# Latent cross-attention on Trainium2: maxima carried into the next pass, and weights prepared through GpSimd's queue

## The chip, the cores and the metric

The kernel runs on one core of one Trainium2 chip. The metric is the device time of one execution in microseconds (us), the median of several runs. The core's engines are TensorE (PE; PEld is its weight load), VectorE (DVE), ScalarE (ACT), GpSimd (POOL) and SyncE (SP), which here only issues DMAs. Each engine works through its own queue in order and waits on semaphores.

## The reference

One layer with 512 latent tokens of width 512 and a context of 8192 tokens: a layer norm and cross-attention with 16 heads of 64, then a state-space block with its gated MLP, then a mixture of 16 experts with two chosen per token and a shared expert. The change concerns the cross-attention and the weights that later parts need:

```python
q = (scale * (Q @ Wq + bq)).reshape(bs, q_len, NH, DM)
k = (K @ Wk + bk).reshape(bs, kv_len, NH, DM)
v = (V @ Wv + bv).reshape(bs, kv_len, NH, DM)
qk = jnp.einsum('nlhd,nshd->nhls', q, k)
a = jax.nn.softmax(qk, axis=-1)
o = jnp.einsum('nhls,nshd->nlhd', a, v).reshape(bs, q_len, NH * DM)
return o @ Wo + bo
```

All inputs are float32. The kernel keeps each factor as two float16 parts, high and low, and multiplies three of the four products.

## The kernel before

The heads are taken in eight pairs, two pairs to a pass, so four passes. A pass goes over the context in 16 chunks of 512 tokens. Per chunk it projects K for both pairs (kproj_units, tile psk, L250 to L252) and V (vproj_units, tile psv, L274 to L276), stores them to device memory (k_d, v_d), and one chunk later computes coarse scores (smax_units, tile psx, L297), which ACT brings to sf (L302) and DVE folds into a running maximum runm (L310). At the end of a pass maxrow_units reduces runm (L317, L318), transposes it on PE (tile ptm, L321), and writes its negative as an extra row of the query tile (mrow, L323, L325).

The attention itself runs in units: a pair of heads and half of the queries, 16 units of 32 steps. A step (scores, then av) takes 256 context tokens: eight matmuls for scores (L359, L360), exponentials on ACT (L367, L369, or in every second step a cast on DVE, L371), the low part by a subtraction on DVE (tile phl, L372, once per step), and the products with V (L389, L392) one or two steps later.

The first pass runs alone. The other three passes are a generator, filler(), whose pieces are woven between the steps of the units before. Every piece yields its nominal cost in ns, and advance() takes pieces until a target is reached: start + LEAD + (n + 0.5) * rate, and again with n + 1.0, where n is the step. So LEAD is how much of the next pass is done before the first step, and rate how much per step. PASSN is the nominal cost of one pass, 223640 ns. Inside filler(), side is a list of score generators, and pump() takes one piece from the first of them, after every second projection piece (every fourth in the first pass). At the end of a pass, before, the list is emptied at once:

```python
            while side:
                yield from pump()
            mr = [maxrow_units(p, runm[i]) for i, p in enumerate(pr)]
            for x in mr:
                yield next(x)
```

The rest of maxrow_units runs in the next pass's first chunk. The order of PE's instructions is the order in which the program writes them. For the other engines and the DMA queues a scheduler of the compiler decides the order, from its own estimate of when each instruction's inputs are ready.

weight_prep() runs beside all this. It first stores zeros to the expert buffers (23 stores to xd_d, L513, and five to y_d, L515), then prepares 52 blocks of weights for the later parts. A block is one load of 512 KB (tile mpf, two buffers, L522) and two halves. Each half is scaled to the high part (L535) and to the low part (L536) on DVE into the tile mph and stored (256 KB, L537). Every second step takes one piece of it. The mph tiles share four buffers (tag t2k) with zero and the projected queries. All these DMAs are issued by SP, whose queue also has the context loads (ctxc, L242), the K and V stores (k_d, L260; v_d, L283) and the loads of K and V for the steps (k, kb, v, L338 to L342).

Steps over NFILL use a second pair of PSUM buffers for scores. The last unit runs beside the beginning of the later parts (tail()).

Of the kernel before, what the change touches and what calls it, by code (L numbers as in the profile page):

```python
# [8 lines left out]
F16 = mybir.dt.float16  # L9
# [7 lines left out]
P = 128  # L17
# [4 lines left out]
CH = 512  # L22
# [7 lines left out]
NPASS = NPAIR // 2  # L30
NDC = NCH // 2
HQ = NQ // 2
NSTEP = 32
PASSN = 16 * (4 * 2592 + 8 * 406) + 2 * 2592 + 600


@with_exitstack
def perceiver_layer(ctx: ExitStack, tc: tile.TileContext, a: dict, out: bass.AP):
    nc = tc.nc
# [96 lines left out]
    sb2 = R(attn, "a2", 2)  # L136
# [146 lines left out]
        nc.sync.dma_start(v_d[g][c // 2][:, tt : tt + 2], vs)  # L283
        yield 648

    def smax_units(c, qh, kh, runm, wide):

        for q2 in range(2):
            sf = sb3.tile([P, 2, 2, CH], F16, name="sf", bufs=2)
            pss = []  # L290
            for qi in range(2):
                qt = 2 * q2 + qi
                for hh in range(2):
                    s = slice(hh * 64, hh * 64 + 64)
                    pool, tag = (ps_s, "pss") if wide and qi else (ps_x, "px")
                    ps = pool.tile([P, CH], F32, name="psx", tag=tag)
                    nc.tensor.matmul(ps, lhsT=qh[s, qt * P : (qt + 1) * P], rhs=kh[s, 0, :], start=True, stop=True)  # L297
                    pss.append((sf[:, qi, hh, :], ps))
                if wide and not qi:
                    continue  # L300
                for dst, ps in pss:
                    nc.scalar.activation(dst, ps, AF.Copy, scale=1.0 / (8.0 * WS))  # L302
                pss = []
                if not qi:
                    yield 406
            r = runm[:, 2 * q2 : 2 * q2 + 2]
            if c == 0:
                nc.vector.tensor_copy(r, sf)
            else:
                nc.vector.tensor_tensor(r, r, sf, ALU.max)  # L310
            yield 626 if wide else 406

    def maxrow_units(p, runm):
        qlm = state[p]["q"][1]
        m = sb2.tile([P, 2, 4], F32, name="mx")
        for w in (256, 128):
            nc.vector.tensor_tensor(runm[:, :, :, 0:w], runm[:, :, :, 0:w], runm[:, :, :, w : 2 * w], ALU.max)  # L317
        nc.vector.tensor_reduce(m.rearrange("p h q -> p q h"), runm[:, :, :, 0:128], axis=AX.X, op=ALU.max)  # L318
        yield 0
        pt = bank_j([P, P], F32, "ptm")  # L320
        nc.tensor.transpose(pt[0:8, :], m.rearrange("p h q -> p (h q)"), ident)  # L321
        r = sb2.tile([8, P], F16, name="mrow")
        nc.scalar.activation(r, pt[0:8, :], AF.Copy, bias=PSHIFT, scale=-1.0)  # L323
        for hh in range(2):
            nc.sync.dma_start(  # L325
                qlm[64:65, hh, :].rearrange("o (a b) -> o a b", b=P), r[hh * 4 : hh * 4 + 4, :]
            )
        state[p]["ready"] = True
        yield 300
# [91 lines left out]
    def filler():  # L421
        side = []

        def pump():
            while side:
                u = next(side[0], None)
                if u is not None:
                    yield u
                    break
                side.pop(0)  # L430

        def pass_weights(g):
            pr = (2 * g, 2 * g + 1)
            out = []
            for src, n, tag, bufs in (
                (a["Wk"][pr[0]], P, "k", 4), (a["Wk"][pr[1]], P, "k", 4), (a["Wv"][g], 256, "v", 2),
                (a["Wq"][pr[0]], P, "q", 2), (a["Wq"][pr[1]], P, "q", 2),
            ):
                w = stage_w(src, n, tag, bufs=bufs)
                yield None  # L440
                out.append(w())
            yield out[0:2], out[2], out[3:5]

        mr, nw = [], None
        for g in range(NPASS):
            pr = (2 * g, 2 * g + 1)
            if g == 0:
                wk0 = load_w(a["Wk"][0], P, "k", bufs=4)
                nct = ctx_first(0)
                wk = [wk0, load_w(a["Wk"][1], P, "k", ("p32", 3), bufs=4)]  # L450
                wv = load_w(a["Wv"][0], 256, "v", ("p32", 3))
                nc.sync.dma_start(x_sb, a["x"])
                wq = [load_w(a["Wq"][p], P, "q", ("t2k", 4)) for p in pr]
            else:
                wk, wv, wq = nw
                qh = [qproj(p, w) for p, w in zip(pr, wq)]
                yield 2 * 2592
            runm = [sb2.tile([P, 4, 2, CH], F16, name=f"runm{i}", tag=f"runm{i}", bufs=1) for i in range(2)] if g else None
            ks = [[None] * NCH for _ in pr]
            for c in range(NCH):  # L460
                if c == NCH - 7 and g < NPASS - 1:
                    nws = pass_weights(g + 1)
                if c >= NCH - 7 and g < NPASS - 1:
                    nw = next(nws, None) or nw
                ct = nct
                nxt = g * NCH + c + 1
                if nxt < NPASS * NCH:
                    nct = ctx_first(nxt) if nxt < NCH else ctx_load(nxt % NCH)
                gens = [kproj_units(p, c, ct, wk[i], ks[i]) for i, p in enumerate(pr)]
                gens += [vproj_units(g, c, ct, wv, j) for j in range(2)]  # L470
                k = 0
                for n, gen in enumerate(gens):
                    for u in gen:
                        yield u
                        k += 1
                        if k % (2 if g else 4) == 0:
                            yield from pump()
                    if mr and c == 0:
                        yield from mr.pop(0)
                if g == 0 and c == 0:  # L480
                    first_norm()
                    qh = [qproj(p, w) for p, w in zip(pr, wq)]
                    yield 2 * 2592
                    runm = [sb2.tile([P, 4, 2, CH], F16, name=f"runm{i}", tag=f"runm{i}", bufs=1) for i in range(2)]
                if c == 2:
                    for p, q in zip(pr, qh):
                        qplace(p, *q)
                side += [smax_units(c, qh[i][0], ks[i][c], runm[i], g == 0) for i in range(2)]
            while side:
                yield from pump()  # L490
            mr = [maxrow_units(p, runm[i]) for i, p in enumerate(pr)]
            for x in mr:
                yield next(x)
            if g == NPASS - 1:
                for x in mr:
                    yield from x
            passes[0] = g + 1

    fill = filler()
# [9 lines left out]
    def weight_prep():  # L509
        zero = sb2.tile([P, 2 * DM], F16, name="zero", tag="t2k", bufs=4)  # L510
        nc.gpsimd.memset(zero, 0.0)
        for k in range(16 + NOV):
            nc.sync.dma_start(xd_d[k * P : (k + 1) * P, :], zero)  # L513
            if k >= 16 + MOV:
                nc.sync.dma_start(y_d[k * P : (k + 1) * P, :], zero.bitcast(F32))  # L515
            if k % 4 == 3 or k == 15 + NOV:
                yield
        blocks = [(name, i, dst) for name in mlp_d for i, dst in enumerate(mlp_d[name])]

        def fetch(j):  # L520
            f = sb2.tile([P, 1024], F32, name="mpf", bufs=2)
            nc.sync.dma_start(f, a[blocks[j][0]][:, blocks[j][1]])  # L522
            return f

        nf = fetch(0)
        yield
        for j, (name, i, dst) in enumerate(blocks):
            f = nf
            if j + 1 < len(blocks):
                nf = fetch(j + 1)  # L530
            yield
            for h in range(2):
                sl = slice(h * 512, h * 512 + 512)
                hl = sb2.tile([P, 2, 512], F16, name="mph", tag="t2k", bufs=4)
                nc.vector.tensor_scalar(hl[:, 0], f[:, sl], WF, None, ALU.mult)  # L535
                nc.vector.scalar_tensor_tensor(hl[:, 1], f[:, sl], WF, hl[:, 0], ALU.mult, ALU.subtract)  # L536
                nc.sync.dma_start(dst[:, :, sl], hl)  # L537
                yield

    ms = ExitStack()  # L540
# [1 line left out]

    units = [(p, h) for p in range(NPAIR) for h in range(2)]
    NLAST = len(units) - 1
    LEAD = 11500
    loads = {}

    def load(j):
# [7 lines left out]
    load(0)  # L556
    advance(start + LEAD)
    load(1)
    pend, enders, early = [], [], weight_prep()
    NFILL = 12 * NSTEP - 4  # L560
    rate = (NPASS - 1) * PASSN / NFILL
    sp = (sb2, sb3, 3)
    po = []

# [10 lines left out]
    for n in range(NLAST * NSTEP):  # L575
# [10 lines left out]
        while len(pend) > (2 if m == 2 else 1):  # L586
            drain()
        advance(start + LEAD + (n + 1.0) * rate)
        pend.append((u, m, cur))
# [769 lines left out]
```

## Time and profile before

| | us |
|---|---|
| median of 3 runs | 2652.26 (2648.97 to 2652.97) |
| profiled execution | 2653.45 |
| its span, first to last instruction | 2651.7 |
| PE busy | 2410.6 (91%) |
| DVE busy | 2049.4 (77%) |
| ACT busy | 1955.5 (74%) |
| POOL busy | 44.2 (2%) |

The granted clock of TensorE has a mean of 0.959 over the span. In the execution that was profiled the first pass ends and the second begins at about 250 us, passes three and four begin near 695 and 1165, and the last projection matmul of pass four starts at 1605; steps run from 278 us. In tables by stretch a row gives a stretch of time, its length, then busy time and number of instructions of each engine, then the granted clock (1.00 is full), the mean busy share of the 16 DMA engines and the rate they moved in GB/s. An idle time in brackets is that of the engine just before the instruction, with what ended it.

### The profile page before, as it was taken

Reading aid. Unit: us, or ns where it says so; the run is one execution under the profiler, and the core shown is the slowest. Engines: PE = TensorE matmul, PEld = TensorE weight load, DVE = VectorE, ACT = ScalarE, POOL = GpSimd, SP = SyncE. Lnnn points to the kernel's source line nnn. Section 1 sums busy time; section 2 is a strip of 40 time slices with the busy share of each in tenths; the row PEclk is TensorE's granted clock in tenths of the full one; section 3 lists DMA queues with packets and bytes.
Section 4 is the critical chain, followed back from the end, with each engine's and each line's share of the span. In section 5 each row is a group of like instructions: output and inputs, shape, how many; then the busy total and the mean of one; then the engine's idle time right before and its main releaser. Section 6 shows DMA issues by size and latency. Waiting matters only on the chain. (4 is left out here: it accounts for less than half of the span.)

```text
span 2651.7 us, 54346 instructions
## 1 busy us (share of the span) xinstructions
PE 2410.6 (91%) x21806; PEld 1693.5 (64%) x21806; DVE 2049.4 (77%) x2403; ACT 1955.5 (74%) x3734; POOL 44.2 (2%) x58
## 2 busy tenths in 40 slices
PE   7999998999999899998999998998878688998895
PEld 4454676777666677766677766997656466665442
DVE  6876688877877877777877777997899999633785
ACT  5787787888787788867788887997868476432784
POOL 2000000000000000000000000000000000001001
PEclk9999999999899999989999998999989889999998
DMA  7973899866598866658966655887511322675896
GB/s 265 308 255 128 268 284 270 242 169 187 166 268 264 265 189 176 184 152 250 253 176 190 173 162 129 201 204 206 171 56 41 96 72 82 229 233 200 294 337 222
DMA packets 353686, 531.42 MB, mean 200 GB/s; under 512 B 25106, under 2 KB 218834, under 8 KB 353300
## 3 DMA queue, kind: packets, MB, share of 16 engines
q1 hardware_dynamic: 352148, 523.69, 65.6%
q0 software_dynamic: 1280, 4.20, 0.5%
q8 instruction: 173, 2.83, 0.5%
q14 instruction: 85, 0.70, 0.1%
HBM read 397.68 MB, written 126.94 MB: 198 GB/s over the span
## 5 line engine op out<-in xcount | busy, mean ns | idle before, releaser
L372 DVE TENSOR_TENSOR phl<-p,phl 128x1024 f16<-128x1024 f32 x512 | 625.9, 1224 | 175.0 <-ACT phl L369 158.9
L367 ACT ACTIVATE p<-pss 128x512 f32<-128x512 f32 x1024 | 596.8, 619 | 126.1 <-PE pss L360 50.7
L302 ACT ACTIVATE sf<-psx 128x512 f16<-128x512 f32 x1024 | 557.7, 622 | 79.1 <-PE psx L297 77.2
L359 PE MATMUL pss<-qhh,k 128*128 128x256 f16 x2048 | 486.2, 277 | 18.5 <-ACT phl L369 18.0
L360 PE MATMUL pss<-qlm,kb 128*128 128x256 f16 x2048 | 485.2, 276 | 0.6 <-DMA kb<-k_d 0.4
L389 PE MATMUL po<-v,phl 128*128 128x130 f16 x4096 | 327.2, 222 | 5.2 <-DVE oq L402 4.7
L310 DVE TENSOR_TENSOR runm<-runm,sf 128x2048 f16<-128x2048 f16 x240 | 292.4, 1218 | 45.7 <-ACT sf L302 45.2
L389 PEld LDWEIGHTS <-phl 128*128 128x128 f16 x4096 | 273.9, 99 | 69.4 <-issue 21.5
L369 ACT ACTIVATE phl<-pss 128x512 f16<-128x512 f32 x512 | 312.3, 610 | 0.0
L274 PE MATMUL psv<-wh_v,ctxc 128*128 128x256 f16 x1024 | 283.4, 277 | 7.7 <-DVE khl L258 3.4
L275 PE MATMUL psv<-wl_v,ctxc 128*128 128x256 f16 x1024 | 282.2, 276 | 1.2 <-DVE wl_v L176 1.2
L276 PE MATMUL psv<-wh_v,ctxc 128*128 128x256 f16 x1024 | 282.1, 276 | 0.0
L359 PEld LDWEIGHTS <-k 128*128 128x128 f16 x2048 | 202.2, 99 | 63.7 <-issue 18.0
L360 PEld LDWEIGHTS <-kb 128*128 128x128 f16 x2048 | 202.7, 99 | 61.0 <-issue 22.2
L297 PE MATMUL psx<-khl,qh 64*128 64x512 f16 x1024 | 212.5, 395 | 21.3 <-ACT sf L302 18.4
L371 DVE CAST phl<-p 128x1024 f16<-128x1024 f32 x256 | 176.1, 688 | 58.1 <-ACT p L367 57.7
L392 PE MATMUL po<-v,phl 128*128 128x65 f16 x4096 | 209.9, 194 | 9.3 <-DVE phl L372 9.3
L250 PE MATMUL psk<-ctxc,wh_k 128*128 128x512 f16 x512 | 198.6, 388 | 21.1 <-DVE vs L281 10.5
L919 PE MATMUL py<-hs,ident 128*128 128x256 f32 x512 | 148.1, 447 | 67.1 <-DVE hs L916 67.0
L251 PE MATMUL psk<-ctxc,wh_k 128*128 128x512 f16 x512 | 197.2, 385 | 0.7 <-DVE ctxc L234 0.7
L252 PE MATMUL psk<-ctxc,wl_k 128*128 128x512 f16 x512 | 196.8, 384 | 0.0
L392 PEld LDWEIGHTS <-phl 128*128 128x128 f16 x4096 | 172.8, 98 | 12.8 <-DVE phl L372 12.0
(304 smaller groups left out, 3711.9 us busy)
## 6 DMA issues: line engine op xcount, KB each, us to landing
v<-v_d SPq DMA_DIRECT2D x128, 520.0 KB, 4.4
k<-k_d SPq DMA_DIRECT2D x256, 256.0 KB, 5.8
ctxc<-ctx_d SPq DMA_DIRECT2D x96, 512.0 KB, 5.2
wef<-in_gu_dram SPq DMA_DIRECT2D x72, 512.0 KB, 5.9
v_d<-vs SPq DMA_DIRECT2D x128, 260.0 KB, 3.8
k_d<-khl SPq DMA_DIRECT2D x128, 256.0 KB, 4.2
kb<-k_d SPq DMA_DIRECT2D x128, 256.0 KB, 5.4
wpm<-w_d SPq DMA_DIRECT2D x48, 512.0 KB, 3.9
```

What stands on the lines that cost most here:

```text
L274: nc.tensor.matmul(ps[:, t, :], lhsT=ct[i // 2][:, 0, i % 2, sl], rhs=wh[:, i, :], start=i == 0, stop=False)
L275: nc.tensor.matmul(ps[:, t, :], lhsT=ct[i // 2][:, 0, i % 2, sl], rhs=wl[:, i, :], start=False, stop=False)
L276: nc.tensor.matmul(ps[:, t, :], lhsT=ct[i // 2][:, 1, i % 2, sl], rhs=wh[:, i, :], start=False, stop=i == NC4 - 1)
L302: nc.scalar.activation(dst, ps, AF.Copy, scale=1.0 / (8.0 * WS))
L310: nc.vector.tensor_tensor(r, r, sf, ALU.max)
L359: nc.tensor.matmul(ps[:, hh], lhsT=k[:, hh, sl], rhs=qhh[:, hh, qs], start=True, stop=False)
L360: nc.tensor.matmul(ps[:, hh], lhsT=b[:, hh, sl], rhs=qlm[:, hh, qs], start=False, stop=True)
L367: nc.scalar.activation(p32[:, i], pss[i], AF.Exp, scale=sc)
L369: nc.scalar.activation(ph[:, i], pss[i], AF.Exp, scale=sc)
L372: nc.vector.tensor_tensor(pl, p32, ph, ALU.subtract)
L389: nc.tensor.matmul(o, lhsT=ph[:, i, hh, qs], rhs=vv, start=first, stop=False, **kw)
L392: nc.tensor.matmul(o, lhsT=pl[:, i, hh, qs], rhs=vv_, start=False, stop=last, **kw)
```

## The change

The drain at the end of a pass is gone: what is left in side, and the two maxrow_units, are carried into the next pass, where one piece is pumped after every projection piece as long as more than two generators wait. runm is allocated by the first score piece of a pass that uses it, since the old maxima may still be in use when the new pass begins. maxrow_units gives three empty pieces between its reduction and its transpose. After the last pass the remaining pieces are spread by LAST / 10 ns each. LEAD rises from 11500 to 27500, NFILL falls by two, and rate follows from both: 1765.6 before, 1723.3 ns per step after. The loads and stores of the weight blocks are issued by GpSimd; the zeros stay with SP. No instruction of PE, DVE or ACT is added or removed.

```diff
+LAST = 8000
...
-    def smax_units(c, qh, kh, runm, wide):
-
+    def smax_units(c, i, qh, kh, runm, wide):
+
+        if c == 0:
+            runm[i] = sb2.tile([P, 4, 2, CH], F16, name=f"runm{i}", tag=f"runm{i}", bufs=1)
...
-            r = runm[:, 2 * q2 : 2 * q2 + 2]
+            r = runm[i][:, 2 * q2 : 2 * q2 + 2]
...
-    def maxrow_units(p, runm):
+    def maxrow_units(p, i, runm):
+        runm = runm[i]
...
-        yield 0
+        for _ in range(3):
+            yield 0
         pt = bank_j([P, P], F32, "ptm")
...
-        mr, nw = [], None
+        nw = None
...
-            runm = [sb2.tile([P, 4, 2, CH], F16, name=f"runm{i}", tag=f"runm{i}", bufs=1) for i in range(2)] if g else None
+            runm = [None, None]
...
                     for u in gen:
                         yield u
                         k += 1
-                        if k % (2 if g else 4) == 0:
+                        if k % (2 if g else 4) == 0 or len(side) > 2:
                             yield from pump()
-                    if mr and c == 0:
-                        yield from mr.pop(0)
...
-                side += [smax_units(c, qh[i][0], ks[i][c], runm[i], g == 0) for i in range(2)]
-            while side:
-                yield from pump()
-            mr = [maxrow_units(p, runm[i]) for i, p in enumerate(pr)]
-            for x in mr:
-                yield next(x)
+                side += [smax_units(c, i, qh[i][0], ks[i][c], runm, g == 0) for i in range(2)]
+            side += [maxrow_units(p, i, runm) for i, p in enumerate(pr)]
             if g == NPASS - 1:
-                for x in mr:
-                    yield from x
+                while side:
+                    yield from pump()
+                    yield LAST / 10
...
-            nc.sync.dma_start(f, a[blocks[j][0]][:, blocks[j][1]])
+            nc.gpsimd.dma_start(f, a[blocks[j][0]][:, blocks[j][1]])
...
-                nc.sync.dma_start(dst[:, :, sl], hl)
+                nc.gpsimd.dma_start(dst[:, :, sl], hl)
...
-    LEAD = 11500
+    LEAD = 27500
...
-    NFILL = 12 * NSTEP - 4
-    rate = (NPASS - 1) * PASSN / NFILL
+    NFILL = 12 * NSTEP - 6
+    rate = ((NPASS - 1) * PASSN + LAST - LEAD) / NFILL
```

More of the change, by code (lines that the diff above doesn't have):

```diff
@@ L483, in filler @@
                     yield 2 * 2592
-                    runm = [sb2.tile([P, 4, 2, CH], F16, name=f"runm{i}", tag=f"runm{i}", bufs=1) for i in range(2)]
                 if c == 2:
```

## The prediction

> **What bounds the kernel now.** I read the page first, then the busy time by stretch, then the same stretches for one line that runs once per step, then the waits of VectorE and the order of time around one of them. The page says that TensorE (PE) is the engine to watch:
>
> ```profile
> PE 2410.6 (91%) x21806; PEld 1693.5 (64%) x21806; DVE 2049.4 (77%) x2403; ACT 1955.5 (74%) x3734; POOL 44.2 (2%) x58
> ```
>
> The busy time by stretch shows where PE is not full. I cut at the places where the three fill passes begin and end (columns: PE, PEld, DVE, ACT, POOL busy, granted clock, DMA share, GB/s):
>
> ```profile
> 250.00:278.00 28.00, 25.84 (x115) 11.68 (x115) 20.02 (x26) 13.91 (x28) 0.00 (x0) 0.82 0.29 105
> 278.00:500.00 222.00, 213.78 (x2171) 153.20 (x2170) 180.58 (x228) 181.02 (x353) 0.00 (x0) 0.98 0.92 280
> 500.00:675.00 175.00, 174.72 (x1823) 126.87 (x1822) 131.68 (x147) 151.12 (x298) 0.00 (x0) 1.00 0.65 182
> 675.00:700.00 25.00, 20.57 (x145) 11.12 (x143) 19.66 (x19) 19.24 (x37) 0.00 (x0) 0.73 0.44 128
> 700.00:925.00 225.00, 206.72 (x2088) 148.36 (x2085) 181.17 (x250) 164.67 (x322) 0.00 (x0) 0.97 0.85 256
> ...
> 1150.00:1175.00 25.00, 22.88 (x162) 12.61 (x161) 19.52 (x24) 15.73 (x30) 0.00 (x0) 0.73 0.34 86
> 1175.00:1325.00 150.00, 136.35 (x1375) 98.82 (x1373) 114.91 (x156) 107.71 (x210) 0.00 (x0) 0.97 0.89 249
> 1325.00:1600.00 275.00, 274.06 (x2875) 200.34 (x2874) 204.46 (x227) 234.49 (x462) 0.10 (x1) 1.00 0.63 175
> 1600.00:1632.00 32.00, 24.11 (x196) 15.73 (x195) 23.94 (x24) 22.30 (x45) 2.19 (x5) 0.73 0.32 82
> ```
>
> The same stretches for L372 alone (one per step) give the pace:
>
> ```profile
> 278.00:500.00 222.00, 75.47 (x62) 0.98 0.92 280
> 500.00:675.00 175.00, 62.76 (x52) 1.00 0.65 182
> 675.00:700.00 25.00, 4.90 (x4) 0.73 0.44 128
> 700.00:925.00 225.00, 71.91 (x59) 0.97 0.85 256
> ...
> 1175.00:1325.00 150.00, 47.92 (x40) 0.97 0.89 249
> 1325.00:1600.00 275.00, 98.52 (x82) 1.00 0.63 175
> ```
>
> Undisturbed, a step takes 175/52 = 3.37 or 275/82 = 3.35 us, PE full and its clock at 1.00: PE sets the pace, 3.36 us. Against it two kinds of stretch lose time. Ends of passes: 25 - 4 x 3.36 = 11.6 us at 675, 25 - 5 x 3.36 = 8.2 at 1150 (five steps there). Weight preparation (L535 and L536 run in no other stretches): 222 - 62 x 3.36 = 13.7, 225 - 59 x 3.36 = 26.8, 150 - 40 x 3.36 = 15.6, together 56 us. There VectorE (DVE) stands still for loads in the middle of its queue:
>
> ```profile
> L535 DVE TENSOR_SCALAR mph<-mpf 128x512 f16<-128x512 f32 x104 | 41.4, 422 | 60.5 <-DMA mpf<-in_w_dram 24.2 <-DMA mpf<-in_Wo_dram 11.1 <-DMA mpf<-in_rsu_dram 10.8
> ```
>
> The order of time around 852 us shows why a load is late: SyncE's queue (SP), then DVE.
>
> ```profile
> 851.95 0.32 SPq L283 DMA_DIRECT2D v_d<-vs  x1
> 852.37 0.57 SPq L342 DMA_DIRECT2D v<-v_d  x1
> 852.99 1.12 SPq L522 DMA_DIRECT2D mpf<-in_w_dram  x1
> ```
> ```profile
> 859.51 0.43 DVE L535 TENSOR_SCALAR mph<-mpf 128x512 f16<-128x512 f32 x1 [2.80 <-DMA mpf<-in_w_dram]
> ```
>
> The mpf buffer was free from about 850.1 us, the load stood behind a v_d store that waits for DVE itself, left at 852.99 and landed 6.5 us later.
>
> **Carried maxima (LEAD, LAST).** PE, DVE and ACT do the same instructions; only places change. In before, the last chunk's eight score pairs run in a row at a pass's end, each needing two evictions by ACT, then the row maxima on DVE, and PE waits.
> First pass's end: 16 L297 take 7.93 us from 250.07 where 16 x 0.216 (their spacing at full clock) is 3.5, so 4.5 lost; the first ten query matmuls at 0.43 instead of 0.216 lose 2.1; two waits of 0.81 for mrow lose 1.6. Sum 8. Second and third: 11.6 and 8.2, above. Afterwards the eight pairs and the maxima alternate with projection groups of the next pass's first chunk; ACT then needs 1.6 pairs x 1.0 + 3 x 0.5 = 3.1 us a step (0.5 us an eviction, 156.16/313 in the stretch after 1632), still under 3.36. So I count all 28 as saved.
> Last pass's end: no projection is left as cover. Before, 1605.3 to 1631.2 (25.9 us) hold the eight pairs, the maxima and five steps, one PE wait of 3.55 us for mx among them. After, LAST spreads pairs over 5.6 steps (406 + 800 = 1206 against a rate of 1723 per step); ACT bounds them at 1.43 x 1.0 + 1.5 = 2.9 us, 16.4 us in all, and the maxima (on DVE 2 x 3.1 us) cost up to 6 more beside a DVE that is 94% busy in the stretch after. Saved 4 to 10, taken 6. If ACT's work there is not hidden, up to 8 us (eight pairs x 1.0) come back at each pass. Sum of the part: 34 us, less 2 for that: 32.
> LEAD moves 16 us of PE work ahead of the first step and takes 42 ns off each of 378 steps: nothing by itself, as PE is full in both places. What it costs if its cover goes: during it DVE and DMA must keep up, see next part. Cost of a gap on PE is doubled by the clock: 0.73 granted at each end of a pass.
>
> **Preparation through GpSimd's queue (POOL).** It takes 52 loads and 104 stores, 0.6 us each, off SP. That time is worth nothing: in its row of groups PE waits 0.4 us for kb, and no longer wait of PE for k, v or ctxc is listed. What counts is when the loads leave, and where DVE's queue puts the preparation. On POOL, a load stands only behind the two stores of the block two before, which wait for DVE's halves that free its buffer anyway. POOL has nothing else until the tail's memsets, long after. The two first loads go out at the start, ahead of the x_sb additions and beside DMA at 0.77: 1 MB, at most 4 us, and they no longer run at 138 us where the share is 0.99. I take 0.
> But the compiled order of the changed program packs the blocks closer on DVE: 16 blocks within LEAD and the first 11 steps (before: 15 over steps 18 to 54), 19.5 in steps 112 to 144 (before 21 in 118 to 172), 14.25 in steps 240 to 264 (before 14 in 244 to 282). At PE's pace these take 27.5 + 16 x 3.32 = 81, 32 x 3.32 = 106 and 24 x 3.32 = 80 us, 267 us for 49.75 blocks, about 48 beyond the two loaded early. Three ends bound the real time.
> DVE alone: undisturbed it is busy 204.46/82 = 2.49 us a step; a half block is 0.42 + 0.68 = 1.10. Steps 112 to 144: 2.5 + 39/32 x 1.10 = 3.84 us; 240 to 264: 2.5 + 28.5/24 x 1.10 = 3.81; the first 16: 2.5 + 15/16 x 1.10 = 3.53. Loss against 3.32: 17 + 12 + 3 = 32 us, DVE being the bound (at least 17 if its instructions overlap by 0.08 as in the order of time).
> DMA alone: undisturbed a step takes 0.63 x 275/82 = 2.1 us of all 16 engines; a block (0.85 x 225 - 59 x 2.16)/21 = 3.0 to (0.89 x 150 - 40 x 2.16)/13.5 = 3.5. At a share of 0.95: (32 x 2.16 + 19.5 x 3.25)/0.95 = 139, loss 33; (24 x 2.16 + 14.25 x 3.25)/0.95 = 103, loss 23; in the first, with 18 us of zero stores (28 of 256 KB at the 400 GB/s that slices after 275 reach) and 15 of LEAD's own traffic (two chunks, 4.1 MB at 280 GB/s), (18 + 15 + 34.6 + 45.5)/0.95 = 119, loss 38. Sum 94.
> The chain of one block: two buffers, DVE holds one about 5 us, then POOL issues (nearest row: its indirect DMAs L1198, 0.95 us) up to three DMAs, and the load lands 4.1 to 8.2 us after issue (median 6.8 on SP). A block then takes from (5 + 1 + 4.1)/2 = 5.1 to (5 + 3 + 8.2)/2 = 8.1 us.
> Per block the ends are 5.1 (no bound), (267 + 32)/48 = 6.2, (267 + 94)/48 = 7.5 and 8.1. I take 6.8, midway between DVE's and DMA's, since in before the share already stood at 0.85 to 0.92 there: loss 6.8 x 48 - 267 = 59 us, against 56 before. Net cost 3.
> By the Trainium skill (DMA: Bandwidth & Descriptors, Issuing engines are not separate DMA queues) another issuing engine saves sequencer time only; that would make this part 0 at the same packing, and the trace's 2.80 us wait behind a blocked store says that order matters too. The Trainium skill (SBUF — State Buffer, Who interferes with whom) warns that descriptors for GpSimd's DMAs are held up while VectorE runs a two-port copy, cast or tensor_scalar, which speaks against this change; no run here shows it, and an estimate of one L371 (0.69 us) per issue would lengthen a block's period by 3 x 0.69/2 = 1 us, to 7.8, and turn the sum into 2671.
>
> **Sum.** 2653.45 (the profiled execution; span 2651.7) - 32 + 3 = 2624.5; the median is 1.2 lower: 2623, given as 2624.
>
> **Rivals.** A, forecast: block period 6.3 to 7.3, loss 35 to 83, 2599 to 2647. B, larger gain: loads are in time and only DVE bounds the packed steps, loss 17 to 32: 2652 - 32 - 39 to - 24 = 2581 to 2596; for it, the 60.5 us of DVE idle before L535 that go; against it, the packing. C, slower: the packed preparation becomes the new wait. DVE stops in its queue at the L535 of each block, in LEAD and at the two starts of a pass, until POOL's load lands; everything queued behind (phl, khl, vs, runm) is late, PE waits, and its clock falls. Break-even is (267 + 56 + 32)/48 = 7.4 us a block, and it decides from 7.5; at 7.7 the loss is 103 and the time 2652 - 32 + 47 = 2667, at 8.1 it is 122 and 2686. For it: DMA share already 0.92 with a looser order; against: loads no longer wait behind SP. D, no change: 7.3 to 7.5 us a block (2647 to 2657), or the maxima only move their waits to ACT.
>
> **Chances.** A 0.46, B 0.17, C 0.28, D 0.09. A measurement of this kernel can tell about 0.2% from no change. The whole of A and B is faster: 0.63; D 0.09; C 0.28. The range leaves out half of B and the outer third of C: 2588 to 2670. A's own range is 2599 to 2647.
>
> **What would show it.** Right: no stretch with a clock of 0.73 at a pass's start, no L297 chain, one wait on mx gone; 3.32 us a step outside preparation. Three packed stretches at about 6.8 us a block, idle before the tensor_scalar of mph near 60 us again but shared among fewer steps. Wrong: block periods over 7.4, or a DMA share near 1.0 in LEAD with PE idle (C); idle before mph under 20 us (B); a pass start still at a low clock (D).

## The result and the profile after

The changed kernel is slower: 2670.71 us, the median of five runs (2663.83 to 2674.33), against 2652.16 for the kernel before in the same measurement. The ratio is 1.0076 with a 95% interval of 1.006 to 1.0093. The forecast was 2624, so it erred by 47 us and in the sign; what came is the rival that it had called C. The profiled execution of the changed kernel has a span of 2664.7 us, 13 more than before, and a higher mean clock, 0.969 against 0.959.

The page's row of TensorE has lost 10 us of busy time, though the kernel got longer:

```profile
PE 2400.8 (90%) x21806; PEld 1685.6 (63%) x21806; DVE 2049.6 (77%) x2403; ACT 1948.8 (73%) x3734; POOL 150.4 (6%) x214
```

The busy time by stretch, cut where preparation runs and where it does not (columns as before: PE, PEld, DVE, ACT, POOL busy, granted clock, DMA share, GB/s):

```profile
300.00:375.00 75.00, 60.55 (x558) 41.40 (x558) 60.05 (x85) 49.00 (x95) 19.48 (x30) 0.93 0.96 316
375.00:675.00 300.00, 297.54 (x3121) 216.75 (x3119) 222.43 (x247) 252.85 (x499) 0.00 (x0) 1.00 0.63 181
675.00:700.00 25.00, 24.44 (x256) 18.01 (x255) 20.76 (x27) 21.20 (x41) 1.93 (x3) 1.00 0.71 204
700.00:850.00 150.00, 126.82 (x1222) 88.01 (x1221) 126.10 (x184) 99.19 (x196) 40.65 (x62) 0.94 0.93 288
...
1150.00:1175.00 25.00, 24.53 (x259) 18.41 (x257) 20.36 (x27) 18.97 (x37) 2.52 (x4) 1.00 0.71 192
1175.00:1275.00 100.00, 84.40 (x799) 57.76 (x798) 82.35 (x122) 63.51 (x127) 27.38 (x39) 0.93 0.87 268
1275.00:1600.00 325.00, 321.99 (x3389) 236.59 (x3388) 241.00 (x264) 274.94 (x542) 0.00 (x0) 1.00 0.62 178
```

The same stretches for L377 (L372 before, once per step; DVE busy and count):

```profile
300.00:375.00 75.00, 20.70 (x17) 0.93 0.96 316
375.00:675.00 300.00, 108.24 (x90) 1.00 0.63 181
...
700.00:850.00 150.00, 43.50 (x37) 0.94 0.93 288
850.00:1150.00 300.00, 108.44 (x89) 1.00 0.62 177
...
1175.00:1275.00 100.00, 27.31 (x23) 0.93 0.87 268
1275.00:1600.00 325.00, 118.75 (x97) 1.00 0.62 178
```

Two things are read here. The starts of passes three and four (now near 690 and 1164), which showed a clock of 0.73 before, now show 1.00 with PE nearly full: the carried maxima did what the prediction said at these places. The three stretches in which POOL is busy, that is, where blocks are prepared, have become the hole. A step is 1.223 us of L377, so 43.50 are 35.6 steps, where 150 us without loss hold 44.5. At 3.37 us a step (925 us / 274 steps in the three quiet stretches) the losses are 75 - 16.9 x 3.37 = 18, 150 - 35.6 x 3.37 = 30 and 100 - 22.3 x 3.37 = 25 us.

In LEAD's stretch the first score came at 297.5, 44.8 us after the second pass had begun. LEAD is 27.5, but that is a nominal cost: in e9_late_sp (below), where no preparation falls into it, the same stretch takes 38.0, so some 7 us are lost here. In 25-us slices before and around the first score:

```profile
275.00:300.00 25.00, 19.30 (x125) 10.68 (x124) 15.33 (x27) 14.81 (x27) 7.90 (x12) 0.99 1.00 342
300.00:325.00 25.00, 16.46 (x121) 9.91 (x121) 17.40 (x27) 13.44 (x26) 6.84 (x11) 0.86 1.00 369
```

The DMA engines are full and PE idles: the sign given for rival C. In VectorE's queue the order of time shows the preparation standing for its own DMAs, once for a store that must free an mph buffer, once for a load:

```profile
285.02 0.43 DVE L534 TENSOR_SCALAR mph<-mpf 128x512 f16<-128x512 f32 x1 [3.04 <-DMA inp_d<-mph]
299.04 0.43 DVE L534 TENSOR_SCALAR mph<-mpf 128x512 f16<-128x512 f32 x1 [2.21 <-DMA mpf<-in_inp_dram]
```

In the whole kernel VectorE's idle time before L534, the first multiplication of each half, is 64.9 us, against 60.5 before:

```profile
L534 DVE TENSOR_SCALAR mph<-mpf 128x512 f16<-128x512 f32 x104 | 42.2, 425 | 64.9 <-DMA mpf<-in_w_dram 26.9 <-DMA mpf<-in_rsu_dram 9.6 <-DMA mpf<-in_inp_dram 7.0
```

That is hardly more, but it now falls into some 370 us in place of 600, and there VectorE has hardly any other idle time. All that it waits for between 700 and 850 us (total us, times, longest):

```profile
DVE mph L534 <- DMA mpf<-in_w_dram: 20.7, 10, 3.5
DVE mph L534 <- DMA mpf<-in_rsg_dram: 3.1, 1, 3.1
```

and its three largest waits in the kernel before, 700 to 925 us, where it also waits for ACT, that is, has time to spare:

```profile
DVE mph L535 <- DMA mpf<-in_w_dram: 20.8, 10, 5.4
DVE phl L372 <- ACT phl L369: 9.6, 8, 3.0
DVE phl L371 <- ACT p L367: 8.2, 6, 2.4
```

### The profile page after: what moved, and what is told of

Its sections match the earlier page's. It is cut to its first block, busy times and chain, and to the rows that moved or that the text cites. A ratio compares the mean times of both kernels' runs of the same rounds, so it can differ in the third digit from the quotient of the medians.

```text
span 2664.7 us, 54475 instructions
## 1 busy us (share of the span) xinstructions
PE 2400.8 (90%) x21806; PEld 1685.6 (63%) x21806; DVE 2049.6 (77%) x2403; ACT 1948.8 (73%) x3734; POOL 150.4 (6%) x214
## 3 DMA queue, kind: packets, MB, share of 16 engines
q0 software_dynamic: 17088, 58.73, 6.5%
## 5 line engine op out<-in xcount | busy, mean ns | idle before, releaser
L377 DVE TENSOR_TENSOR phl<-p,phl 128x1024 f16<-128x1024 f32 x512 | 626.0, 1224 | 209.5 <-ACT phl L374 199.6
L372 ACT ACTIVATE p<-pss 128x512 f32<-128x512 f32 x1024 | 599.3, 624 | 158.9 <-PE pss L365 77.9
L275 PE MATMUL psv<-wh_v,ctxc 128*128 128x256 f16 x1024 | 284.3, 278 | 13.5 <-DVE khl L259 5.2
L251 PE MATMUL psk<-ctxc,wh_k 128*128 128x512 f16 x512 | 198.5, 388 | 16.2 <-ACT ctxc L234 8.2
```

The source lines that it names most:

```text
L275: nc.tensor.matmul(ps[:, t, :], lhsT=ct[i // 2][:, 0, i % 2, sl], rhs=wh[:, i, :], start=i == 0, stop=False)
L372: nc.scalar.activation(p32[:, i], pss[i], AF.Exp, scale=sc)
L377: nc.vector.tensor_tensor(pl, p32, ph, ALU.subtract)
```

## The experiments

All were timed in five rounds against the kernel before on the same chip. "Step" is the difference to the kernel before, from the ratio times 2652. "Idle" is VectorE's idle time, in us over the whole profile, before the first multiplication of each of the 104 halves (the expectations call these the first halves); the kernel before has 60.5.

| run | preparation's DMAs | median us | ratio (95%) | step | idle |
|---|---|---|---|---|---|
| after | GpSimd | 2670.71 | 1.0076 (1.006 to 1.0093) | +20 | 64.9 |
| e1_sp | SP | 2619.04 | 0.9894 (0.9869 to 0.9919) | -28 | 42.8 |
| e2_pool (before) | GpSimd | 2694.75 | 1.0162 (1.0135 to 1.0189) | +43 | 74.3 |
| e3_paced | GpSimd | 2662.76 | 1.0049 (1.0025 to 1.0073) | +13 | 175.0 |
| e4_paced_sp | SP | 2616.7 | 0.9874 (0.985 to 0.9899) | -33 | 88.9 |
| e6_loads_pool | loads GpSimd | 2660.46 | 1.0032 (1.0017 to 1.0047) | +8 | 169.3 |
| e7_stores_pool | stores GpSimd | 2617.68 | 0.9874 (0.9854 to 0.9893) | -33 | 77.8 |
| e8_late_pool | GpSimd | 2596.63 | 0.979 (0.9769 to 0.9812) | -56 | 1.9 |
| e9_late_sp | SP | 2593.75 | 0.9781 (0.976 to 0.9801) | -58 | 1.9 |
| e10_loads_sp | stores GpSimd | 2627.86 | 0.9913 (0.9889 to 0.9937) | -23 | 33.9 |
| e11_stores_sp | loads GpSimd | 2650.39 | 0.9992 (0.998 to 1.0004) | -2 | 50.8 |
| e12_use_spread | GpSimd | 2597.18 | 0.9798 (0.9775 to 0.9822) | -54 | 2.0 |
| e13_before_late (before) | SP | 2605.37 | 0.9822 (0.9799 to 0.9845) | -47 | 2.4 |
| e14_lead20 | SP | 2593.95 | 0.9783 (0.9761 to 0.9805) | -58 | 2.9 |
| e15_lead40 | SP | 2585.03 | 0.9745 (0.9727 to 0.9764) | -68 | 1.7 |

**The two parts alone.** e1_sp is the changed kernel with the preparation's queue undone, e2_pool the kernel before with that queue alone changed:

```diff
-            nc.gpsimd.dma_start(f, a[blocks[j][0]][:, blocks[j][1]])
+            nc.sync.dma_start(f, a[blocks[j][0]][:, blocks[j][1]])
...
-                nc.gpsimd.dma_start(dst[:, :, sl], hl)
+                nc.sync.dma_start(dst[:, :, sl], hl)
```

> The changed kernel with the loads and stores of the weight blocks issued by SP again; carried maxima, LEAD, LAST and rate stay as changed. Theory P (packing): GpSimd's empty queue let the compiler's scheduler pull the preparation together, and the packed stretches cost all of the loss; with SP the order of VectorE has 16 blocks over steps 0 to 48 again, so the loss of the packed stretches falls from 84 us to about 55 and the carried maxima show their gain of 15 to 32: 2620 to 2640. Theory M (the carried maxima themselves, or the 16 us of extra LEAD, cost more than they save): 2655 or more. Theory Q (a DMA issued by GpSimd is slow in itself): same as P here.

> The kernel before with only the queue changed: loads and stores of the weight blocks issued by GpSimd; the drain at a pass's end, LEAD and rate stay as before. Its order on VectorE is packed as in the changed kernel (14.75 blocks in the first 16 steps, 20 in steps 112 to 144). Theory P: the drains at the passes' ends stay (34 us) and the packed stretches cost 75 to 90 in place of 56: 2670 to 2690, the slowest of all. Theory M: the queue is not what costs, 2645 to 2660. Theory Q: 2670 to 2690 as well.

Measured: 28 us faster and 43 us slower than before, the one just under and the other just over its expected range. The change is a gain and a loss laid over each other, and the queue is the loss: 43 us on the old order of passes, 48 (from -28 to +20) on the new one. What remained was why: because GpSimd's empty queue lets the compiler's scheduler draw the blocks together, or because of the queue itself.

**The same spread on both queues.** e3_paced spreads the blocks evenly: ahead of each load VectorE copies one column of the current step's phl into the buffer, so the load waits for that step. In the trace the 52 blocks then lie between steps 14 and 316, about 20 us apart. e4_paced_sp is the same on SP's queue.

```diff
             f = sb2.tile([P, 1024], F32, name="mpf", bufs=2)
+            if pace:
+                nc.vector.tensor_copy(f[:, 0:1], pace[0][:, 0, 0, 0:1])
...
         pend.append((u, m, cur))
+        pace[:] = [cur[2]]
```

> The changed kernel, GpSimd's queue kept, but each load of a weight block has to wait for a step: VectorE copies one column of that step's exponentials into the buffer before the load (52 instructions of about 0.1 us). The order on VectorE then has 2 to 3 blocks per 16 steps from the first unit to the tenth, nowhere more. Theory P: no stretch with more than 0.85 of DMA share, VectorE's idle time before the tensor_scalar of mph under 15 us, a step at 3.36 us throughout, loss 84 us down to 10 or less: 2590 to 2605. Theory Q: GpSimd's descriptors cost at any pace; at least a third of the loss stays and VectorE still waits for the loads: 2630 or more. Theory M: 2600 to 2650, and the LEAD stretch still has PE idle.

> As the paced kernel before it in this list, but with the loads and stores on SP. The order on VectorE is the same to the block. Theory P: within 6 us of the paced kernel on GpSimd's queue, either way. Theory Q: faster than that one by 15 us or more. A rival of P that only looks at SP (a load on SP stands behind a store that waits): VectorE waits for loads again, 30 us or more before the tensor_scalar of mph, and the time is 15 us or more above the paced kernel on GpSimd.

Measured: 2662.76 and 2616.7, 46 us apart, though no stretch is packed in either. So it was not the packing alone. The groups of VectorE between 250 and 1600 us show where the time lies, in e3_paced (after the second bar: idle us just before the group, and what ended it):

```profile
L377 DVE TENSOR_TENSOR phl<-p,phl 128x1024 f16<-128x1024 f32 x365 | 445.0, 1223 | 83.0 <-ACT phl L374 75.7 <-PE psx L300 1.7
```
```profile
L537 DVE TENSOR_SCALAR mph<-mpf 128x512 f16<-128x512 f32 x104 | 40.3, 424 | 175.0 <-DMA mpf<-in_w_dram 73.8 <-DMA mpf<-in_inp_dram 24.5 <-DMA mpf<-in_Wo_dram 21.4
```

and in e4_paced_sp:

```profile
L377 DVE TENSOR_TENSOR phl<-p,phl 128x1024 f16<-128x1024 f32 x378 | 461.7, 1224 | 121.1 <-ACT phl L374 114.1 <-PE psx L300 1.7
```
```profile
L537 DVE TENSOR_SCALAR mph<-mpf 128x512 f16<-128x512 f32 x104 | 40.8, 424 | 88.9 <-DMA mpf<-in_w_dram 33.1 <-DMA mpf<-in_Wo_dram 16.4 <-DMA mpf<-in_inp_dram 9.4
```

VectorE stands 86 us longer for loads on GpSimd's queue; 38 us of that it would else have waited for ACT's exponentials, and the remaining 48 are the difference in time. An instruction takes as long in both (424 ns, 1223 and 1224 ns): it is waiting, not slower work. One block in the order of time of e3_paced:

```profile
598.79 0.14 DVE L523 CAST mpf<-phl 128x1 f32<-128x1 f16 x1
598.85 0.69 DVE L376 CAST phl<-p 128x1024 f16<-128x1024 f32 x1
...
599.23 0.55 POOL L524 DMA_DIRECT2D mpf<-in_w_dram  x1 [8.85 <-DVE mpf L523]
599.57 1.23 DVE L377 TENSOR_TENSOR phl<-p,phl 128x1024 f16<-128x1024 f32 x1
608.02 0.76 DVE L537 TENSOR_SCALAR mph<-mpf 128x512 f16<-128x512 f32 x2 [7.23 <-DMA mpf<-in_w_dram]
609.90 1.22 DVE L377 TENSOR_TENSOR phl<-p,phl 128x1024 f16<-128x1024 f32 x1
```

The load leaves at 599.23 and VectorE has two instructions of other work until it needs it; it then stands for 7.23 us, and the next step's L377 comes at 609.90, 10.3 us after the last. In e4_paced_sp a block at about the same time:

```profile
589.17 0.14 DVE L523 CAST mpf<-phl 128x1 f32<-128x1 f16 x1
589.28 0.69 DVE L376 CAST phl<-p 128x1024 f16<-128x1024 f32 x1
590.01 1.22 DVE L377 TENSOR_TENSOR phl<-p,phl 128x1024 f16<-128x1024 f32 x1
...
594.75 0.75 DVE L259 SCALAR_TENSOR_TENSOR khl<-psk,bk_sb,khl 128x512 f16<-128x512 f32 x1
595.41 1.22 DVE L313 TENSOR_TENSOR runm<-runm,sf 128x2048 f16<-128x2048 f16 x1
596.54 0.69 DVE L376 CAST phl<-p 128x1024 f16<-128x1024 f32 x1
598.10 0.43 DVE L537 TENSOR_SCALAR mph<-mpf 128x512 f16<-128x512 f32 x1 [0.87 <-DMA mpf<-in_w_dram]
```

Here six instructions stand between (one is left out above), and 0.87 us is left to wait. In e3_paced at most three instructions stand between the copy ahead of the load and the use in 36 of 52 blocks, in e4_paced_sp in 26. In time, VectorE does 3.2 us of other work between a load's issue and its use in e3_paced, 4.4 in e4_paced_sp (means over 52 blocks): that is some 60 of the 86 us. The other 26 are a longer time from issue to use, 6.6 us against 6.1; in the 38 blocks in which VectorE stood in both runs it was 6.4 against 5.7. (The landing itself is in the trace for all 52 loads of GpSimd, but for only three of those of SP, too few to compare.)

**Loads or stores.** If the wait for the load is the price (theory T), the 104 stores may stay on GpSimd. Each run takes one of the two kinds off e3_paced's queue.

> The evenly spread order of e3_paced, with the 52 loads on GpSimd's queue as there and the 104 stores back on SP's. Theory T: what costs is the load's time from issue to landing on GpSimd's queue, because VectorE takes its instructions in order and stands at the first multiplication of a block until the load lands (175 us in e3_paced against 82 in e4_paced_sp). T expects e3_paced's time, 2655 to 2668, and 150 to 190 us of VectorE idle before the first halves. Rival S (the stores hold up the loads on the queue): near e4_paced_sp, 2612 to 2625, idle about 80. Rival D (each DMA that GpSimd issues costs the same in itself, for whatever reason): a third of the 46 us, some 2632.

> The same order, with the loads on SP's queue and the 104 stores on GpSimd's. T expects e4_paced_sp's time, 2612 to 2625, since nothing waits for a store but the next use of its buffer, and VectorE idle before the first halves about 80 us. S has no say on it beyond that. D expects two thirds of the 46 us, some 2647.

Measured: 2660.46 and 2617.68, as T expected and neither a third nor two thirds. Of e6_loads_pool and of e7_stores_pool the group of these first multiplications:

```profile
L537 DVE TENSOR_SCALAR mph<-mpf 128x512 f16<-128x512 f32 x104 | 40.2, 423 | 169.3 <-DMA mpf<-in_w_dram 61.3 <-DMA mpf<-in_inp_dram 24.3 <-DMA mpf<-in_Wo_dram 21.4
```
```profile
L537 DVE TENSOR_SCALAR mph<-mpf 128x512 f16<-128x512 f32 x104 | 40.8, 423 | 77.8 <-DMA mpf<-in_w_dram 28.2 <-DMA mpf<-in_Wo_dram 15.7 <-DMA mpf<-in_rsd_dram 10.1
```

In this spread order 104 stores, two thirds of the DMAs and half the bytes, cost nothing on GpSimd; 52 loads carry it all.

**A later use.** The loads stay on GpSimd in e8_late_pool, but each half also waits for a step, so that some 30 instructions of VectorE lie between a load and its use:

```diff
                 hl = sb2.tile([P, 2, 512], F16, name="mph", tag="t2k", bufs=4)
+                nc.vector.tensor_copy(hl[:, 0, 0:1], pace[0][:, 0, 0, 0:1])
```

> e3_paced (both kinds on GpSimd's queue), and each half's multiplication also waits for a step of the attention (a copy of one column into mph ahead of it, 104 times some 0.15 us of VectorE), so that about two pairs of steps lie between a load and its use. T: the wait for loads goes (under 20 us idle before the first halves in all) and the loss with it: within 10 us of e9_late_sp, 2610 to 2632. D, or a port theory in which VectorE and GpSimd's descriptors hold each other up: 35 to 50 us above e9_late_sp.

> The same late use with loads and stores on SP's queue. T: idle before the first halves falls from 82 us to under 20; part of it was covered by other waits of VectorE, so the time is at e4_paced_sp's 2617 or up to 25 under it, less up to 15 us for the 104 small copies where VectorE is the bound: 2600 to 2622.

Measured: 2596.63 and 2593.75. Idle time before the first multiplications is 1.9 us in both (e8_late_pool's row):

```profile
L538 DVE TENSOR_SCALAR mph<-mpf 128x512 f16<-128x512 f32 x104 | 44.1, 424 | 1.9
```

The 46 us between the queues are gone, or 3 at most: the intervals overlap. Both runs are faster than I had expected (2610 to 2632, and 2600 to 2622): the 89 us of idle time that SP's queue had left were not as well hidden as I took them to be, and the 104 small copies cost nothing that shows.

**Back to the changed kernel.** In e10 to e12 the loads are not spread by hand. e10_loads_sp takes the loads off GpSimd's queue and e11_stores_sp the stores; e12_use_spread keeps both on it and adds only the copy ahead of each half.

> The changed kernel with the 52 loads on SP's queue and the 104 stores left on GpSimd's; nothing is spread by hand, so the blocks stay drawn together as in the changed kernel (most of them within the first two 16 steps, less dense than there). If the loads' path through GpSimd is the greater part of the changed kernel's loss, it comes down by 25 us or more, to 2630 to 2645. If the packing is (VectorE full, whoever issues), it stays within 12 us of the changed kernel, 2658 to 2675.

> The changed kernel with the loads left on GpSimd's queue and the stores on SP's; blocks as packed as in the run with the loads on SP. If the loads' path counts: 2655 to 2675, as the changed kernel, and above the run with the loads on SP by 20 us or more. If packing counts alone: equal to that run within 8 us.

> The changed kernel with one addition: ahead of each half's multiplication a copy of one column of the current step's phl into mph, so that the halves are spread over the steps; loads are left to go as early as their buffer allows, and loads and stores stay on GpSimd's queue. If only the moment of use counts: as e8_late_pool, 2590 to 2605. If GpSimd's queue costs anything by itself: 10 us or more above that.

Measured: 2627.86, 2650.39, 2597.18. The first two are a little under what I had expected. Against the changed kernel's +20, taking the loads away is worth 43 us, the stores 22, both (e1_sp) 48, so they overlap. I had expected nothing of the stores alone. With either kind on SP the blocks lie less close (8.2 and 8.8 us a block in the first stretch, 6.6 in the changed kernel), and the waits for loads fall from 58 us to 32 and 34. The waits for a store to free an mph buffer do not explain what the stores cost, since they rise from 6 to 16 us with the stores on SP. The rows of e10_loads_sp and of e11_stores_sp:

```profile
L534 DVE TENSOR_SCALAR mph<-mpf 128x512 f16<-128x512 f32 x104 | 41.7, 423 | 33.9 <-DMA mpf<-in_w_dram 16.0 <-DMA mpf<-in_rsu_dram 4.1 <-DMA mpf<-in_rsd_dram 3.7
```
```profile
L534 DVE TENSOR_SCALAR mph<-mpf 128x512 f16<-128x512 f32 x104 | 42.2, 420 | 50.8 <-DMA w_d<-mph 9.5 <-DMA mpf<-in_w_dram 8.8 <-DMA mpf<-in_rsu_dram 8.6
```

e12_use_spread adds only the copy, and 74 us of the medians go. Queue and DMAs are as they were; but the copy ties the halves to steps 17 to 323, and with them the loads, so it takes away the waits (64.9 to 2.0 us) and the packing together. L377 between 300 and 1600 us, first in the changed kernel, then in e12_use_spread:

```profile
300.00:1600.00 1300.00, 442.85 (x362) 0.98 0.70 207
```
```profile
300.00:1600.00 1300.00, 469.00 (x384) 0.99 0.74 216
```

22 steps more in the same time, 22 x 3.37 = 74 us.

How much is the packing and how much the waits, no single run separates, but the six kernels without added copies show how they meet. "Lost" is the difference in "step" to the same kernel with spread loads and late use (e13_before_late for the first and last row, e9_late_sp for the others), "us a block" the first stretch of preparation divided by its blocks:

| kernel | us a block | idle | lost |
|---|---|---|---|
| before | 12.2 | 60.5 | 47 |
| e1_sp | 11.0 | 42.8 | 30 |
| e11_stores_sp | 8.8 | 50.8 | 56 |
| e10_loads_sp | 8.2 | 33.9 | 35 |
| after | 6.6 | 64.9 | 78 |
| e2_pool | 6.6 | 74.3 | 90 |

A microsecond of VectorE's waiting goes with 0.7 to 0.8 us lost where the blocks lie loosely and with 1.2 where they lie closest; in e4_paced_sp and e3_paced, at 20 us a block, with 0.3 and 0.4. This is a comparison of kernels that differ in more than one thing, and no test of the packing by itself.

**The maxima without the preparation's waits.** e13_before_late puts the spread loads and late use into the kernel before; e9_late_sp is the same with the carried maxima, LEAD and LAST.

> The kernel before with the spread loads and late use of e9_late_sp, all on SP's queue: it differs from e9_late_sp only in the carried maxima, the later start and the last pass. The prediction gave these 32 us, e1_sp 28: so 22 to 36 us above e9_late_sp's 2594, 2616 to 2630. If the gain at the pass starts came only through the preparation's place there, it is under 12 us above it.

Measured: 2605.37, only 12 us above e9_late_sp (11 by the ratios), where the prediction's 32 and e1_sp's 28 had led me to expect 22 to 36; that is at the edge of the other reading, under 12. The dips at the starts of passes are there in e13_before_late and gone in e9_late_sp, whose passes begin earlier (one row of each):

```profile
675.00:700.00 25.00, 21.70 (x160) 12.15 (x158) 20.47 (x26) 15.85 (x30) 0.00 (x0) 0.80 0.42 110
```
```profile
650.00:675.00 25.00, 25.00 (x258) 17.82 (x256) 22.09 (x32) 20.59 (x40) 0.00 (x0) 1.00 0.82 258
```

So part of what they give comes back elsewhere. Between the two traces the first score comes 13.5 us later, the time from there to the last projection is 15.6 us shorter, and the end up to the last product 10.1 us shorter. It is the middle that falls short: the 16 us that LEAD takes off the steps and the 20 of two pass ends would make 36. One reading was that LEAD's longer start is lost time. e14_lead20 and e15_lead40 are e9_late_sp with another LEAD alone:

```diff
-    LEAD = 27500
+    LEAD = 20000
```

> e9_late_sp with LEAD 20000 in place of 27500 (rate follows). The prediction held that LEAD costs nothing, because what is done ahead is taken off the steps: then the same time within 5 us, 2589 to 2599. The other reading (N): the steps do not get shorter, as the 3.37 us measured in the changed kernel suggests, and LEAD is lost time: some 7 us less, 2583 to 2590.

> e9_late_sp with LEAD 40000. As the prediction held: the same time within 5 us. N: 12 us more, 2602 to 2612.

Measured: 2593.95 and 2585.03. A shorter LEAD changes nothing and a longer one is 9 us faster, so that reading falls. Where the other 16 to 20 us of the maxima's gain went is not settled. e15_lead40 is the fastest version of all, 2.5% below the kernel before and 3.2% below the changed one.

## Why the prediction was wrong

The step that failed is the term "Preparation through GpSimd's queue": a period of 6.8 us a block, hence a loss of 59 against 56 and a net cost of 3 us. Undoing this part alone (e1_sp) moved the time by 48 us. The other term, the carried maxima, was predicted at 32 us and gave 28 with the old queue. So the one term holds nearly all of the error, and it turned the sign.

It was wrong on both sides of its difference. The packed preparation lost 80 us in place of 59: 18 + 30 + 25 in the three stretches and 7 in LEAD; the distance from e9_late_sp gives 78. That is (267 + 80)/48 = 7.2 us a block, or 7.4 if all of LEAD beyond its nominal 27.5 is counted, as the prediction's 267 does: neither reaches the 7.5 from which it let rival C decide, so that C's time came only in part for C's reason. The other part is that the 56 us of the kernel before did not stay: beside the carried maxima the old queue's preparation costs only 30 (e1_sp to e9_late_sp). Both 78 and 30 are counted from e9_late_sp, so their difference is the 48 above, where the prediction had 59 - 56.

In the packed preparation's own price, what was wrong is not the packing, which came as the compiled order had shown, but the choice of the middle. I priced VectorE's work and the DMA engines' work as two bounds and took their midpoint. VectorE is not a pool of capacity but a queue in order: when it stands for a load, its own work behind that load is late as well, so waits add to work.

By the rows above VectorE is idle for 15 + 24 + 18 = 57 us in the three packed stretches, nearly all of it before the preparation's own halves, and 73 us are lost: at most 57 by waits, and at least 16 by VectorE's own work, which no longer fits beside PE's pace. (The prediction's bound for VectorE's work alone was 32.) The row of 60.5 us idle before was read as a thing to go or to stay "near 60 us again"; it stayed (64.9) and was right as a forecast, yet its price changed, since before, half of VectorE's idle time in the preparation's stretches (58 of 120 us) was for the loads, and much of the rest for ACT: time to spare.

Nor did the room for a load shrink. From its issue to its use VectorE started 7 other instructions in the median block before and 7.5 after, too few both times (32 in e12_use_spread, where the waits are gone). What the change made earlier is the issue: 0.9 us after the buffer was free, where on SP's queue it was 9.7. The loads took longer in the packed stretches, 7.3 us to landing in the median against 5.6 in e3_paced and e8_late_pool, at a DMA share of 0.87 to 0.96; how much of the waits that is, no run separates. The 4.1 to 8.2 us that the prediction took for a load from SP are those of seven of 52 loads, the only ones whose landing that trace shows.

The sum also took the 56 us of the kernel before as fixed. With spread loads and late use the kernel before gains 47 (e13_before_late): nearly all of them could be had, by an edit that has nothing to do with queues.

The carried maxima came near their 32 us, and the trace agrees with the places: clock 1.00 at the pass starts, and from the last projection to the last product 301.8 us in e1_sp in place of 309.1, where 6 had been predicted. But e13_before_late against e9_late_sp gives only 11 to 12. The two parts are not separate: spread loads and late use gain 47 us on the kernel before and 30 on e1_sp, so some 17 of e1_sp's 28 are preparation that loses less beside the carried maxima. The prediction added its terms as though they were separate.

The predicted 3.32 us a step outside preparation was 3.37. Most of that lies in the 3.36 it started from, which counts steps that a stretch's edge cuts as whole ones. By busy time, as for 3.37 above, the kernel before takes 675 us / 198.5 steps = 3.40, with the third quiet stretch of L372:

```profile
925.00:1150.00 225.00, 81.68 (x67) 1.00 0.65 181
```

So a step became 0.03 us shorter where 0.04 had been predicted. At 3.40 the preparation of the kernel before lost 55 us, as good as the 56 of the prediction. That LEAD is simply lost was tested and fell.

The Trainium skill (DMA: Bandwidth & Descriptors, Issuing engines are not separate DMA queues) says that a different issuing engine saves sequencer time only, not transfer time. e8_late_pool and e9_late_sp agree within 3 us where nothing waits on the load. e3_paced and e4_paced_sp differ by 46 with the blocks spread alike: the rule speaks of transfers, and most of that time was in where VectorE's order puts the use behind the load (60 of 86 us of waiting), the rest in loads that took some 0.7 us longer. The warning that speaks against the change (SBUF — State Buffer, Who interferes with whom), that VectorE's two-port instructions hold up GpSimd's descriptors, would have given 2671, by chance the measured time. The runs do not show it at work: e8_late_pool has the same VectorE instructions and GpSimd DMAs, and loses nothing that shows. Whether it has a part in the 0.7 us, or in the 9.7 us of the slowest load of e3_paced, was not tried.

## What to carry to other kernels

Before moving a DMA to another queue, look at what its consumer's engine does in the meantime: count the instructions between the load's issue and its first use on that engine, times their duration, and compare with the landing times of the trace. If the room is short, an engine that works in order stands, and everything behind it is late. What that costs depends on whether the engine has other idle time in the same stretch: 0.3 us for each microsecond of waiting in the loosest order here, 1.2 in the closest. A cheap data dependency that holds the use back and spreads it (here a copy of one column, 0.15 us) took 74 us off the changed kernel and left 3 between the queues. When two parts of a change touch the same stretch, price them together: each alone may find the same idle time.

## What the runs showed of the hardware

The page counts the DMAs that GpSimd issues in another row: "software_dynamic" went from 4.20 MB in 1280 packets to 58.73 MB in 17088. Loads of 512 KB from GpSimd landed in 5.6 us in the median (3.8 to 9.7) where they were spread and 7.3 (4.7 to 9.9) where they were packed. Where VectorE stood for a load in both e3_paced and e4_paced_sp, it took 6.4 us from issue to use from GpSimd and 5.7 from SP; with late use the queues made no difference in time beyond 3 us. The issue of a load occupied GpSimd for 0.56 to 0.69 us in the median of a run, that of a store for 0.68; 104 stores issued there cost the kernel nothing where the blocks were spread (e7_stores_pool). With the DMA share at 1.00 the core moved 342 to 369 GB/s.
